# Layer 3, near tiles: VectorE masks all of the first pair of heads while ScalarE copies from the second, then both change banks

## The chip, the core and the metric

The kernel runs on one core of a Trainium2 chip. The metric is the time of one execution on the device in microseconds, the median of several. The core has five engines with queues of their own, each of which works strictly in the order in which its instructions were issued: TensorE (PE, with its weight loads shown apart as PEld), VectorE (DVE), ScalarE (ACT), GpSimd (POOL) and SyncE (SP), which issues the transfers. TensorE writes its results to PSUM, from where VectorE and ScalarE take them to SBUF.

## The reference

Four layers over x of shape (4, 256, 48, 48). Each adds to x a function of its group-normalised self; layers 0 to 2 are convolutions. The change is in layer 3, a linear attention over windows with 8 heads of 32 channels, for three window sizes:

```python
q = sigmoid(Wq x);  k = sigmoid(Wk x);  v = (Wv x) / |Wv x|      # per head
Ik, Ikv = integral(k), integral(k v^T)       # sums over rows and columns
for w in (1, 2, 4):                          # window of 48/w by 48/w pixels
    wk, wkv = box(Ik, 48 // w), box(Ikv, 48 // w)
    attn = einsum("bdhw,bdfhw->bfhw", q, wkv)
    norm = einsum("bdhw,bdhw->bhw", q, wk)
    outs.append(attn / (norm + 1e-6))
out = Wout concat(outs) + bout
```

The kernel doesn't form `k v^T` for each pixel. It computes the products q.k of a block of queries with a block of keys, sets to zero those in which the key lies outside of the query's window (the masks), and multiplies by v. One such product with three masks serves the three windows. The windows nest: with half sizes of 24, 12 and 6 pixels, everything in the smallest lies in the middle one, and everything in that lies in the widest.

## The kernel before

A tile is a block of 8 rows of keys (`a`) with one of three groups of 16 columns (`c`), 128 keys in all, against a block of 8 rows of queries (`rb`). There are 720 tiles in the kernel's order. Four heads are worked on in a tile, as two pairs. The scores of a pair fill a PSUM tile of two banks, one for each head; there are two such tiles, one for each pair, so that the scores of the next tile's first pair have to wait until the first pair of this one has been read.

```python
HALVES = [24, 12, 6]          # W // w // 2
LAG = 2

# ps_s: bufs=2, space=PSUM;   smp: bufs=2 * (LAG + 1)
def scores(self, pr, a, c):
    ...
    s = ps_s.tile([P, 2, 512], F32, tag="s", name="s")
    for j in range(2):
        head = slice((2 * pr + j) * D, (2 * pr + j + 1) * D)
        pe.matmul(s[:, j, 0 : (r1 - r0) * (c1 - c0)],
                  kvs[self.b, self.ct, a][0][head, c, :],
                  self.qs[head, r0:r1, c0:c1], start=True, stop=True)
    ...

def masked(self, a, c, ss):
    ...
    def of_banks(s, tiles, wi, rows, cols):      # VectorE: PSUM times mask -> SBUF
        src = s[:, :, rows[0] - r0 : rows[1] - r0, cols[0] - c0 : cols[1] - c0]
        times_mask(dve, wi, rows, cols, view(tiles, wi, rows, cols), src)

    f0, f1 = max(0, c * KC + KC - HALVES[0]), min(W, c * KC + HALVES[0] + 1)
    full = abs(a - rb) * RB + RB <= HALVES[0]    # no row of the widest window is cut
    many = seen(NW - 1, a, rb)                   # the smallest window reaches this tile

    def middle(s, tiles):                        # VectorE, the middle window
        if full and many:
            of_banks(s, tiles, 1, rows_seen(1, a, rb), cols_seen(1, c))

    def copy(s, tiles):                          # ScalarE, where the widest mask is all ones
        if full:
            act.copy(view(tiles, 0, (r0, r1), (f0, f1)), s[:, :, :, f0 - c0 : f1 - c0])

    def widest(s, tiles):                        # VectorE, the rim of the widest window
        if not full:
            of_banks(s, tiles, 0, *all0)
            return
        for p0, p1 in ((c0, f0), (f1, c1)):
            if p0 < p1:
                of_banks(s, tiles, 0, (r0, r1), (p0, p1))

    first, second = zip(ss, pairs)
    copy(*first)
    middle(*second)
    copy(*second)
    middle(*first)
    widest(*first)
    widest(*second)
    for tiles in pairs:                          # GpSimd, from what was copied to SBUF
        wi = NW - 1 if many else 1
        if wi in wis:
            rows, cols = rows_seen(wi, a, rb), cols_seen(wi, c)
            src = view(tiles, 0, rows, cols)
            times_mask(pool, wi, rows, cols, view(tiles, wi, rows, cols), src)
    ...

# the main loop: scores and masks of tile n, then the sums over keys of tile n - 2
for n in range(len(stream) + LAG):
    if n < len(stream):
        ...
        ss = [blocks[i].scores(pr, a, c) for pr in range(NPR)]
        ahead.append(blocks[i].masked(a, c, ss))
        ...
    if n >= LAG:
        ...
        for wi in (1, 0, 2):
            if wi in sms[0]:
                blocks[i].sums(wi, a, c, sms)    # TensorE: acc += v^T sm
        ...
    advance()       # a step of each side job: projections, sums of k, norms, outputs
```

A tile is near when `full and many` holds, that is when its block of rows is that of the queries or a neighbour (384 tiles). In a near tile VectorE makes the middle window and the rim of the widest (one piece for c = 0 and c = 2, two for c = 1), ScalarE copies what no mask cuts, and GpSimd makes the smallest window out of the copy. In 192 more tiles, two rows of blocks away, `full` holds and `many` does not; 144 are not `full`. Near tiles and others alternate as far as there are enough of the latter.

Two engines that read the same PSUM tile do so one after the other, in the order of the program: the framework that places the semaphores orders any two accesses to one bank.

Of the kernel before, what the change touches and what calls it, by code (L numbers as in the profile page):

```python
# [145 lines left out]
def conv_preact_kernel(  # L146
# [306 lines left out]
    with (  # L453
# [975 lines left out]
        with (  # L1429
# [11 lines left out]
            first = ExitStack()  # L1441
# [41 lines left out]
    with (  # L1483
# [187 lines left out]
        def rows_seen(wi, a, rb):  # L1671

            h = HALVES[wi]
            return (
                max(0, a * RB - h + 1 - rb * RB),
                min(RB, a * RB + RB + h - rb * RB),
            )

        def cols_seen(wi, c):
            h = HALVES[wi]  # L1680
            return max(0, c * KC - h + (wi > 0)), min(W, c * KC + KC + h)

        class Block:
# [28 lines left out]
            def masked(self, a, c, ss):  # L1712

                rb = self.rb
                all0 = rows_seen(0, a, rb), cols_seen(0, c)
                (r0, r1), (c0, c1) = all0
                wis = [wi for wi in range(NW) if seen(wi, a, rb)]
                pairs = [
                    {
                        wi: smp.tile(  # L1720
                            [P, 2, RB, min(W, KC + 2 * HALVES[wi])],
                            F32,
                            tag=f"sm{wi}",
                            name=f"sm{wi}",
                        )
                        for wi in wis
                    }
                    for _ in ss
                ]

                def view(tiles, wi, rows, cols):
                    (y0, _), (x0, _) = rows_seen(wi, a, rb), cols_seen(wi, c)
                    return tiles[wi][
                        :, :, rows[0] - y0 : rows[1] - y0, cols[0] - x0 : cols[1] - x0
                    ]

                def times_mask(engine, wi, rows, cols, dst, src):
                    mr = rb * RB + rows[0] - (a * RB - HALVES[wi] + 1)
                    mc = cols[0] - (c * KC - MCOL0[wi])
                    nr, ncol = rows[1] - rows[0], cols[1] - cols[0]  # L1740
                    m = mask[wi][:, mr : mr + nr, mc : mc + ncol]
                    engine.tensor_mul(
                        dst, src, m.unsqueeze(1).to_broadcast([P, 2, nr, ncol])
                    )

                def of_banks(s, tiles, wi, rows, cols):
# [6 lines that stand above are left out]
                full = abs(a - rb) * RB + RB <= HALVES[0]  # L1753

                many = seen(NW - 1, a, rb)

                def middle(s, tiles):
                    if full and many:
                        of_banks(s, tiles, 1, rows_seen(1, a, rb), cols_seen(1, c))

                def copy(s, tiles):
                    if full:
                        act.copy(
                            view(tiles, 0, (r0, r1), (f0, f1)), s[:, :, :, f0 - c0 : f1 - c0]
                        )

                def widest(s, tiles):
# [7 lines that stand above are left out]


                first, second = zip(ss, pairs)
                copy(*first)
                middle(*second)
                copy(*second)  # L1780
                middle(*first)
                widest(*first)
                widest(*second)
                for tiles in pairs:

# [5 lines that stand above are left out]
                return [  # L1791
                    {wi: view(t, wi, rows_seen(wi, a, rb), cols_seen(wi, c)) for wi in wis}
                    for t in pairs
                ]
# [28 lines left out]
        def seen(wi, a, rb):  # L1823
            r0, r1 = rows_seen(wi, a, rb)
            return r0 < r1
# [226 lines left out]
```

## Time and profile before

| | before |
|---|---|
| time, median of 3 runs | 3778.4 us (3774.7 to 3779.35) |
| span of the profiled execution | 3775.4 us |
| mean granted TensorE clock | 0.952 |
| busy: TensorE matmul, weight load | 3264.8 us (86%), 1879.4 us (50%) |
| busy: VectorE, ScalarE, GpSimd | 2487.2 us (66%), 1036.2 us (27%), 1518.1 us (40%) |
| VectorE masks of scores, `sm<-s,masks` | 2592, 1135.8 us busy |
| ScalarE copies of scores, `sm<-s` | 1152, 594.9 us busy |
| GpSimd masks, `sm<-sm,masks` | 1152, 853.3 us busy |

In the profile an instruction's operands carry the program's names: `s` is a PSUM tile of scores, `sm` one of the masked tiles in SBUF, `acc` the sums, `ks`, `qs` and `vs` are keys, queries and values. All instructions stand at one line of the program, L142, the helper that records them, so they are told apart by engine, operands and shape. `x <- y` in a list of waits reads "x sat idle until y was done"; after the colon stand the sum of these waits in us, their number and the longest. An fp32 matmul shows as two records.

### The profile page before, as it was taken

Reading aid. Unit: us, or ns where it says so; the run is one execution under the profiler, and the core shown is the slowest. Engines: PE = TensorE matmul, PEld = TensorE weight load, DVE = VectorE, ACT = ScalarE, POOL = GpSimd, SP = SyncE. Lnnn points to the kernel's source line nnn. Section 1 sums busy time; section 2 is a strip of 40 time slices with the busy share of each in tenths; the row PEclk is TensorE's granted clock in tenths of the full one; section 3 lists DMA queues with packets and bytes.
Section 4 is the critical chain, followed back from the end, with each engine's and each line's share of the span. In section 5 each row is a group of like instructions: output and inputs, shape, how many; then the busy total and the mean of one; then the engine's idle time right before and its main releaser. Section 6 shows DMA issues by size and latency. Waiting matters only on the chain. (4 is left out here: it accounts for less than half of the span.)

```text
span 3775.4 us, 68847 instructions
## 1 busy us (share of the span) xinstructions
PE 3264.8 (86%) x26498; PEld 1879.4 (50%) x26498; DVE 2487.2 (66%) x5119; ACT 1036.2 (27%) x2025; POOL 1518.1 (40%) x2184
## 2 busy tenths in 40 slices
PE   3688898998996788988889889899899899989998
PEld 2467686786784564433334334344443344444443
DVE  7876587587583366777666567756577766556665
ACT  0012111111113322433222333332344332233331
POOL 0000120020020034778765486755365766344332
PEclk9798999999997899999999899999999999999999
DMA  7745323324324313345434243533223444101122
GB/s 250 238 135 170 100 104 116 109 95 125 109 75 124 102 70 108 125 136 159 125 103 131 90 136 122 164 97 108 78 95 123 139 116 116 47 31 53 41 60 60
DMA packets 373019, 423.04 MB, mean 112 GB/s; under 512 B 129076, under 2 KB 328532, under 8 KB 371540
## 3 DMA queue, kind: packets, MB, share of 16 engines
q1 hardware_dynamic: 371491, 416.32, 35.6%
q8 instruction: 211, 3.46, 0.4%
q0 software_dynamic: 144, 1.52, 0.2%
q14 instruction: 117, 0.95, 0.1%
q10 hardware_dynamic: 1056, 0.79, 0.1%
HBM read 288.79 MB, written 131.25 MB: 111 GB/s over the span
## 5 line engine op out<-in xcount | busy, mean ns | idle before, releaser
L142 DVE TENSOR_TENSOR sm<-s,masks 128x112 f32<-128x112 f32 (+10 forms) x2592 | 1135.8, 493 | 765.5 <-PE s L142 321.1
L142 POOL TENSOR_TENSOR sm<-sm,masks 128x432 f32<-128x432 f32 (+14 forms) x1152 | 853.3, 755 | 936.5 <-ACT sm L142 672.0
L142 PE MATMUL s<-qs,ks 32*128 32x320 f32 (+3 forms) x5760 | 832.5, 500 | 200.1 <-DVE sm L142 151.2
L142 ACT COPY sm<-s 128x528 f32<-128x528 f32 (+2 forms) x1152 | 594.9, 535 | 1470.7 <-PE s L142 1169.9
L142 PE MATMUL acc<-sm,vs 128*32 128x384 f32 (+18 forms) x13440 | 880.5, 385 | 16.1 <-POOL sm L142 15.8
L142 PEld LDWEIGHTS s<-qs,ks 32*128 32x128 f32 x5760 | 374.1, 185 | 604.7 <-DVE sm L142 232.8
L142 PE MATMUL cv<-vx,wt 128*128 128x288 f32 x2080 | 559.3, 425 | 90.7 <-DVE vx L142 49.1
L142 PEld LDWEIGHTS acc<-sm,vs 128*32 128x32 f32 x13440 | 355.2, 110 | 551.3 <-issue 348.6
L142 PEld LDWEIGHTS cv<-vx,wt 128*128 128x128 f32 x2080 | 402.4, 198 | 212.4 <-issue 53.6
L142 POOL MEMSET v<- 128x16 f32 (+1 forms) x120 | 18.6, 215 | 725.7 <-DVE vx L142 635.7
L142 PE MATMUL cv<-v,wl 128*128 128x384 f32 x1152 | 224.5, 354 | 24.4 <-DVE x L142 9.2
L142 PEld LDWEIGHTS cv<-v,wl 128*128 128x128 f32 x1152 | 214.8, 195 | 34.6 <-issue 16.1
L142 POOL TENSOR_TENSOR pt<-pt 128x144 f32<-128x144 f32 x336 | 187.4, 558 | 22.8 <-DVE pt L142 0.5
L142 POOL TENSOR_TENSOR v<-l2v,v 128x384 fp32r<-128x384 f32 x96 | 109.2, 1168 | 130.2 <-ACT v L142 121.4
L142 POOL TENSOR_TENSOR nhi<-nhi,nq 128x384 f32<-128x384 f32 x144 | 148.3, 1058 | 0.0
L142 PE MATMUL cv<-pad,wl 128*128 128x384 bf16 x864 | 143.1, 327 | 0.0
L142 PE MATMUL out_ps<-o,wout_sb 128*128 128x384 f32 x288 | 122.8, 509 | 9.4 <-DVE o L142 5.4
L142 PE MATMUL out_ps<-stage,wout_sb 128*128 128x384 f32 x288 | 117.3, 489 | 0.4 <-DVE stage L142 0.4
L142 PE MATMUL proj_ps<-wv_sb,xn 128*128 128x256 f32 x288 | 89.5, 438 | 32.3 <-ACT vt L142 19.1
L142 DVE TENSOR_TENSOR vx<-v 128x868 f32<-128x868 f32 x112 | 115.4, 1056 | 0.5
L142 PE MATMUL ap<-seen,xT 120*128 120x120 f32 (+3 forms) x832 | 113.5, 293 | 0.0
L142 PEld LDWEIGHTS <-wl 128*128 128x128 bf16 x864 | 83.8, 97 | 59.1 <-issue 0.4
(162 smaller groups left out, 2859.0 us busy)
## 6 DMA issues: line engine op xcount, KB each, us to landing
wt<-wt SPq DMA_DIRECT2D x48, 768.0 KB
kb_d<-pt SPq DMA_DIRECT2D x48, 576.0 KB
rc<-r_d SPq DMA_DIRECT2D x192, 144.0 KB
nhi<-kb_d SPq DMA_DIRECT2D x120, 192.0 KB
nlo<-kb_d SPq DMA_DIRECT2D x88, 192.0 KB
o_d<-stage SPq DMA_DIRECT2D x24, 576.0 KB
o<-o_d SPq DMA_DIRECT2D x24, 576.0 KB
wl<-wl_d SPq DMA_DIRECT2D x16, 768.0 KB
```

What stands on the lines that cost most here:

```text
L142: return lambda *args, **kwargs: self.tc.keep_in_program_order(op(*args, **kwargs))
```

## The change

In near tiles the order of the six steps is changed. Before, ScalarE began with the first pair and VectorE with the second, and they changed pairs after one step. Now VectorE does its whole work on the first pair (middle and rim) while ScalarE copies from the second; then ScalarE copies from the first, and VectorE does its whole work on the second. The thought behind it is that VectorE can begin when the first pair's scores are there, without waiting for the second's, and that it comes to be done with the first pair's banks sooner. For the other tiles the order stays what it was: `middle` did nothing there.

```diff
                 first, second = zip(ss, pairs)
-                copy(*first)
-                middle(*second)
-                copy(*second)
-                middle(*first)
-                widest(*first)
+                if full and many:
+                    middle(*first)
+                    widest(*first)
+                    copy(*second)
+                    copy(*first)
+                    middle(*second)
+                else:
+                    copy(*first)
+                    copy(*second)
+                    widest(*first)
                 widest(*second)
                 for tiles in pairs:
```

## The prediction

> **What bounds the kernel now.** I read the page first, then the busy time by stretches, then the chain of waits of the stretch in which layer 3 runs, then one tile of it in order of time. The score matmuls, which the page calls `s<-qs,ks`, run from 1429.5 us to 3751 us, so layer 3's attention lies in the last 2327 us, and only there can the change act. The busy time of that stretch (us; then busy time and number of instructions of PE, PEld, DVE, ACT, POOL; clock, DMA share, GB/s):
>
> ```profile
> core 0: us, PE busy (x) PEld busy (x) DVE busy (x) ACT busy (x) POOL busy (x), PEclk, DMA share, GB/s
> 1429.00:3756.00 2327.00, 2071.52 (x20642) 938.44 (x20642) 1543.81 (x3288) 773.85 (x1537) 1364.18 (x1886) 0.97 0.34 103
> ```
>
> TensorE is busy 89% of it, VectorE 66%, GpSimd 59%, ScalarE 33%. TensorE is idle for 2327.0 - 2071.5 = 255.5 us, and the chain of waits of the same stretch says for whom (total us, times, longest):
>
> ```profile
> POOL sm L142 <- ACT sm L142: 672.0, 468, 18.0
> DVE sm L142 <- PE s L142: 321.1, 342, 9.2
> DVE sm L142 <- ACT sm L142: 266.9, 181, 5.5
> ACT sm L142 <- DVE sm L142: 235.9, 349, 3.8
> PE s L142 <- DVE sm L142: 151.2, 243, 3.9
> PEld acc L142 <- POOL sm L142: 57.7, 118, 3.8
> PE acc L142 <- POOL sm L142: 15.8, 17, 3.3
> PE s L142 <- ACT sm L142: 13.7, 20, 1.4
> ```
>
> The line to see is `PE s <- DVE sm`: 243 times TensorE cannot begin the scores of the next tile, because VectorE is still masking the banks they go into; 151.2 us, 59% of its idle time. GpSimd, which comes last in the masking, holds TensorE back for only 15.8 us. So the loop that sets the pace is scores, masking, release of the banks, next scores.
>
> One near tile in order of time (start, us, engine, operation, count, idle before it and what ended it):
>
> ```profile
> 2821.34 1.29 PE L142 MATMUL s<-qs,ks 32*128 32x384 f32 x8 [0.21 <-DVE sm L142]
> 2821.58 0.80 DVE L142 TENSOR_TENSOR pt<-cs 128x384 f32<-128x384 f32 x1
> 2822.36 0.61 ACT L142 COPY sm<-s 128x528 f32<-128x528 f32 x1 [0.87 <-PE s L142]
> ...
> 2822.75 2.28 DVE L142 TENSOR_TENSOR sm<-s,masks 128x624 f32<-128x624 f32 x6 [0.37 <-PE s L142]
> 2823.05 0.82 POOL L142 TENSOR_TENSOR sm<-sm,masks 128x324 f32<-128x324 f32 x1 [0.21 <-ACT sm L142]
> 2823.65 0.61 ACT L142 COPY sm<-s 128x528 f32<-128x528 f32 x1 [0.68 <-DVE sm L142]
> ...
> 2824.80 1.29 PE L142 MATMUL s<-qs,ks 32*128 32x384 f32 x8 [0.83 <-DVE sm L142]
> ```
>
> The first pair's scores can be read at 2822.36 (ScalarE starts on them), the second pair's at 2822.75 (VectorE starts on them, after 0.37 us of waiting for TensorE). VectorE runs m2, m1, w1, w1, w2, w2 back to back in 2.28 us (m is the middle window, w the rim of the widest, the digit the pair). ScalarE's second copy starts at 2823.65, 0.10 us after m2 is over (2822.75 + 0.80, the duration from the list below): the two engines are never in the same pair's banks together. The next scores start at 2824.80 after 0.83 us of idle TensorE, and the trace has the last w1 end 0.15 us before.
>
> VectorE's masks by shape (count, busy us, mean ns, idle before):
>
> ```profile
> L142 DVE TENSOR_TENSOR sm<-s,masks 128x624 f32<-128x624 f32 x256 | 194.9, 802 | 98.3 <-PE s L142 94.2 <-ACT sm L142 3.2 <-POOL sm L142 0.8
> L142 DVE TENSOR_TENSOR sm<-s,masks 128x448 f32<-128x448 f32 x256 | 147.9, 619 | 89.0 <-PE s L142 87.6 <-ACT sm L142 0.8
> L142 DVE TENSOR_TENSOR sm<-s,masks 128x432 f32<-128x432 f32 x256 | 143.7, 602 | 92.8 <-PE s L142 85.2 <-POOL pt L142 3.6 <-POOL sm L142 3.1
> ```
>
> These three are the middle masks of the three key columns c = 1, 0, 2, two to each near tile: 384 near tiles. Before them VectorE waits 94.2/128 = 0.74, 0.68 and 0.67 us a tile for TensorE. In all of these tiles it begins with the pair that is scored last.
>
> **What the Trainium skill says.** "PSUM — Partial Sum Buffer", section "PSUM bank collisions raise a hardware error", says that no two engines may be in one bank's quadrant at once, two readers included, and that software has to order them. The trace agrees: each `ACT sm <- DVE sm` (349 waits, 235.9 us) is a copy that waits for a mask of the same pair. So in the changed kernel the copy of the first pair has to follow w1, and m2 has to follow the copy of the second. "Perfetto Trace Analysis", section "Identifying the Most-Contended Engine", calls matmul busy time a bad measure of how near an engine is to its limit. Here too: the loads are busy 938 of 2327 us, 40%, while the matmul row shows 89%, and in 482 of the 719 steps from tile to tile the scores start within 0.3 us of VectorE's last mask on their banks. I therefore count waits and not busy shares.
>
> **The change part by part.** Nothing is added or removed: 2592 masks, 1152 copies and 1152 GpSimd products stay, each on its engine and with its shape. Only the order in the 384 near tiles changes. In the other tiles m was empty, so the order there is the same.
>
> For the tile above, with its own durations, the new order gives:
> - VectorE is free at 2821.58 + 0.80 = 2822.38, and the first pair is readable: it starts 0.37 us earlier. m1, w1, w1 are half of 2.28 us: over at 2823.52.
> - ScalarE copies the second pair from 2822.75 to 2823.36. That is before 2823.52, so m2 does not wait. The copy of the first pair starts 0.10 us after w1, at 2823.62, and ends at 2824.23.
> - The first pair's banks are then free, and 0.15 us later, at 2824.38, the next scores start, against 2824.80: 0.42 us earlier. TensorE has been free since 2823.97, so 0.41 of the 0.83 us stay.
> - m2, w2, w2 end at 2824.66 instead of 2825.03. With 0.15 us the second pair's banks are ready at 2824.81; the second scores follow the first by 0.40 us, at 2824.78. The second release takes nothing back.
>
> In general the first release moves from d + m2 + m1 + w1 to d' + m1 + w1 + c1. The gain is (d - d') + m - c - 0.10: the earlier start (about 0.4 us), one m (0.73, 0.56, 0.55 us when pipelined) less one copy (0.61, 0.51, 0.48 us) and one handover. That is 0.40 to 0.45 us with an idle VectorE. Where VectorE is busy with side work when the first pair is ready (a quarter of the tiles by its idle time ahead of m2), d - d' shrinks; c = 0 and 2 lose up to 0.3 us on m2 waiting for the copy. I take 0.35 us.
>
> It counts only where TensorE waits, and no more than the wait. I put the 243 + 20 waits of scores for VectorE and ScalarE beside the order of tiles: behind a near tile there are 86 (c = 1, 79.9 us), 57 (c = 2, 24.6 us) and 11 (c = 0, 9.0 us). The rest, over 100, stand behind other tiles, whose order stays. Taking the smaller of the wait and 0.35 us in each of the 154 gives 30.1 + 19.8 + 3.6 = 53.5 us. Behind the other 230 near tiles TensorE still had sums, projections or outputs to do, so the earlier release is not used.
>
> **What it costs.** GpSimd takes the pairs in the order first, second, and its input is the copy. The first copy now ends last: in the example at 2824.23 instead of 2822.97. GpSimd starts 1.2 us later, and ends near 2825.9 instead of 2825.15, and its own side work waits behind it. The sums that need these products come two tiles later: measured, they start 4 to 6 us (median) after the product is ready, but in 18 of 764 cases less than 1 us. Some 15 to 30 of these may now hold TensorE for 0.3 to 0.5 us: about 8 us. Net: 53.5 - 8 = 45 us, 1.2%: 3778.4 - 45 = 3733, rounded to 3732.
>
> **Rivals.** (a) GpSimd becomes the last wait. For it: its 672 us of waiting for ScalarE shows that it follows the copies closely, and it is 59% busy. Each near tile costs it about 1 us more of blocked time, 384 us in all, and 2327 - 1364 = 963 us are idle. Against it: the margins above. It would eat all of the gain: 3770 to 3800. (b) ScalarE blocks. It now waits for w1 with its first copy in hand, so sigmoid, stage and projection evacuations stand behind it; TensorE waits for these some 50 us today. Against it: the last copy ends at the same time as before (2824.23 against 2824.26). It would cost 10 to 20 us. (c) The whole wait goes: if the earlier VectorE also shortened the waits behind other tiles, up to 100 us might come, 3680. Against it: there the release follows the tile's own copies and masks, which do not move. (d) Nothing: TensorE's rate is the bound and the gain reappears as another wait, 3775. Against it: nearly all transitions start at a release.
>
> **Range and chances.** A gain of 0.25 us instead of 0.35 a wait, with the GpSimd loss doubled, leaves about 20 us; 0.45 us without loss gives 65. Unknown knock-on effects widen this to 3695 to 3775. Over 2% faster (below 3702.8) needs 0.5 us at each of the 154 waits, more than the arithmetic yields: 0.11. Over 2% slower needs GpSimd to take the lead outright: 0.06. Within: 0.83.
>
> **What would show it.** `PE s <- DVE sm` should fall from 151 us to 60 or less; part of it returns as `PE s <- ACT sm`, as a copy now frees the bank, and their sum (165 us) should come down by about 50. `DVE sm <- PE s` should fall from 321 us by about 0.4 us a near tile. `POOL sm <- ACT sm` should rise and `PE acc <- POOL sm` should stay below 30 us; if that reaches 60, rival (a) is right. Durations of masks and copies should not move. I am wrong if the first copy does not follow w1 at 0.1 us, or if the sum of scores' waits stays.

## The result, and the profile after

| | before | after |
|---|---|---|
| time, median of 4 runs each | 3776.55 us (3771.95 to 3779.35) | 3749.91 us (3744.02 to 3755.96) |
| ratio after to before, 95% interval | | 0.9931 (0.9911 to 0.9950) |
| span of the profiled execution, clock | 3775.4 us, 0.952 | 3748.1 us, 0.950 |

The change makes the kernel 26.6 us faster, 0.7%. In a second comparison, below, the ratio was 0.9920.

Layer 3 of the changed kernel by stretches; the first is batches 0 to 2, the second batch 3, cut where the trace has the first scores of a batch (us, busy us and number of instructions of PE, PEld, DVE, ACT, POOL, clock, DMA):

```profile
1422.05:3228.33 1806.29, 1624.76 (x15641) 723.96 (x15641) 1261.61 (x2591) 607.90 (x1210) 1166.03 (x1598) 0.96 0.39 118
3228.33:3722.00 493.67, 478.45 (x4962) 217.23 (x4962) 322.34 (x695) 160.70 (x324) 209.18 (x288) 0.99 0.17 49
```

The same two stretches of before:

```profile
1429.52:3233.67 1804.15, 1598.95 (x15640) 719.89 (x15641) 1228.40 (x2591) 609.88 (x1210) 1156.06 (x1598) 0.97 0.39 118
3233.67:3751.00 517.33, 469.32 (x4956) 217.01 (x4960) 313.19 (x695) 162.53 (x324) 208.13 (x288) 1.00 0.16 47
```

Batch 3 came down by 23.7 us. Batches 0 to 2, with three times as many tiles, came down by nothing (+2.1 us). Ahead of layer 3, where nothing was changed, this pair of traces differs by 7.5 us more, and behind these stretches by 1.7 us the other way: layer 3 began at 1429.5, 1422.0 and, in a third trace, at 1420.6 us, so that part is chance.

The clock plays a part too. The trace lists the phases in which TensorE's clock was halved; half of their length is called lost clock below. I read it as the most that such phases cost. In batches 0 to 2 it was 58.0 us before and 67.7 us after, in batch 3 1.7 and 3.4 us.

The chain of waits of layer 3 after:

```profile
POOL sm L142 <- ACT sm L142: 406.4, 200, 19.4
DVE sm L142 <- ACT sm L142: 296.3, 263, 7.3
DVE sm L142 <- PE s L142: 207.9, 200, 10.4
ACT sm L142 <- DVE sm L142: 98.0, 194, 3.2
PEld acc L142 <- POOL sm L142: 83.3, 142, 5.1
PE s L142 <- ACT sm L142: 66.7, 115, 3.4
PE s L142 <- DVE sm L142: 52.7, 98, 4.6
PE acc L142 <- POOL sm L142: 19.2, 21, 4.6
```

TensorE's waits ahead of scores for VectorE and ScalarE together fell from 151.2 + 13.7 = 164.9 us to 52.7 + 66.7 = 119.4 us. That is 45.5 us less: 30.8 us in batch 3 (from 44.0 to 13.2) and only 14.7 us in batches 0 to 2 (from 120.9 to 106.2). The kernel became less than 30 us faster. The page's own row for the scores tells where a part of the rest is. Before, then after (busy us, mean ns, idle before):

```profile
L142 PE MATMUL s<-qs,ks 32*128 32x320 f32 (+3 forms) x5760 | 832.5, 500 | 200.1 <-DVE sm L142 151.2
```

```profile
L142 PE MATMUL s<-qs,ks 32*128 32x320 f32 (+3 forms) x5760 | 861.2, 500 | 134.8 <-ACT sm L142 66.7
```

The same 5760 records of 500 ns each cover 28.7 us more time: they are stretched apart. One near tile (c = 1, the same in both traces) shows how. Before:

```profile
3329.37 1.29 PE L142 MATMUL s<-qs,ks 32*128 32x384 f32 x8
...
3330.78 2.28 DVE L142 TENSOR_TENSOR sm<-s,masks 128x624 f32<-128x624 f32 x6 [1.09 <-PE s L142]
...
3332.83 1.29 PE L142 MATMUL s<-qs,ks 32*128 32x384 f32 x8 [0.83 <-DVE sm L142]
```

After:

```profile
3318.02 1.20 PE L142 MATMUL s<-qs,ks 32*128 32x384 f32 x8
...
3319.06 2.28 DVE L142 TENSOR_TENSOR sm<-s,masks 128x624 f32<-128x624 f32 x6 [0.80 <-PE s L142]
...
3319.32 0.61 ACT L142 COPY sm<-s 128x528 f32<-128x528 f32 x1 [1.53 <-PE s L142]
3320.28 0.61 ACT L142 COPY sm<-s 128x528 f32<-128x528 f32 x1 [0.34 <-DVE sm L142]
3320.94 1.45 PE L142 MATMUL s<-qs,ks 32*128 32x384 f32 x8 [0.39 <-ACT sm L142]
```

Counted from the tile's own first scores, VectorE begins at 1.04 instead of 1.41 us, and the next scores begin at 2.92 instead of 3.46 us, 0.54 sooner, released by ScalarE's copy. But the group of eight now takes 1.45 instead of 1.29 us. It ends at 4.37 instead of 4.75: 0.38 us sooner, as much as VectorE's last mask. In the trace the second pair's scores start 0.15 us after that mask in both kernels: 0.38 us after the first pair's before, 0.54 us after.

VectorE's middle masks after (count, busy us, mean ns, idle before):

```profile
L142 DVE TENSOR_TENSOR sm<-s,masks 128x624 f32<-128x624 f32 x256 | 205.2, 802 | 71.0 <-PE s L142 59.0 <-ACT sm L142 5.7 <-POOL sm L142 2.8
L142 DVE TENSOR_TENSOR sm<-s,masks 128x448 f32<-128x448 f32 x256 | 158.3, 618 | 60.1 <-PE s L142 43.2 <-ACT sm L142 14.8
L142 DVE TENSOR_TENSOR sm<-s,masks 128x432 f32<-128x432 f32 x256 | 154.0, 602 | 60.6 <-PE s L142 45.8 <-ACT sm L142 9.6 <-POOL pt L142 3.5
```

The mask takes what it took. The wait for the first scores has shrunk from 94.2 to 59.0, 87.6 to 43.2 and 85.2 to 45.8 us, and for c = 0 and 2 (448 and 432 elements) there is now some waiting for ScalarE: m2 for the copy of the second pair.

### The profile page after: what moved, and what is told of

It reads as the page before. It is cut to its first block, busy times and chain, and to the rows that moved or that the text cites. A ratio compares the mean times of both kernels' runs of the same rounds, so it can differ in the third digit from the quotient of the medians.

```text
span 3748.1 us, 69137 instructions
## 1 busy us (share of the span) xinstructions
PE 3291.0 (88%) x26498; PEld 1878.5 (50%) x26498; DVE 2529.4 (67%) x5119; ACT 1032.1 (28%) x2025; POOL 1528.8 (41%) x2184
## 3 DMA queue, kind: packets, MB, share of 16 engines
q8 instruction: 212, 3.47, 0.4%
## 5 line engine op out<-in xcount | busy, mean ns | idle before, releaser
L142 DVE TENSOR_TENSOR sm<-s,masks 128x112 f32<-128x112 f32 (+10 forms) x2592 | 1148.2, 492 | 695.4 <-ACT sm L142 296.3
L142 POOL TENSOR_TENSOR sm<-sm,masks 128x432 f32<-128x432 f32 (+14 forms) x1152 | 881.2, 787 | 910.8 <-ACT sm L142 406.4
L142 PE MATMUL s<-qs,ks 32*128 32x320 f32 (+3 forms) x5760 | 861.2, 500 | 134.8 <-ACT sm L142 66.7
L142 PE MATMUL acc<-sm,vs 128*32 128x384 f32 (+18 forms) x13440 | 886.4, 386 | 19.5 <-POOL sm L142 19.2
L142 DVE TENSOR_TENSOR pt<-cs 128x384 f32<-128x384 f32 x144 | 120.3, 835 | 0.0
L142 DVE SCALAR_TENSOR_TENSOR x<-cv,alpha,x 128x384 f32<-128x384 f32 x144 | 83.9, 610 | 44.6 <-PE cv L142 44.3
```

The costliest lines, as they stand in the source:

```text
L142: return lambda *args, **kwargs: self.tc.keep_in_program_order(op(*args, **kwargs))
```

## The experiments

Each ratio is to the kernel before, run on the same chip. "VectorE's end" is, from the trace, the median over the 384 near tiles of the time from the tile's first scores to the end of VectorE's last mask of it.

| kernel | median us | ratio (95% interval) | VectorE's end, us |
|---|---|---|---|
| before | 3776.1 to 3781.7 | 1 | 3.30 |
| changed, again | 3744.9 | 0.9920 (0.9899 to 0.9942) | 3.10 |
| GpSimd second pair first | 3738.5 | 0.9897 (0.9876 to 0.9918) | 3.08 |
| begin with the first pair only | 3813.9 | 1.0096 (1.0066 to 1.0126) | 3.37 |
| changed order without w2 | 3712.2 | 0.9835 (0.9810 to 0.9860) | 2.86 |
| order of before without w2 | 3731.5 | 0.9874 (0.9846 to 0.9903) | 2.95 |
| mirror image | 3790.6 | 1.0028 (1.0016 to 1.0040) | 3.32 |
| first release later | 3783.1 | 0.9998 (0.9988 to 1.0009) | 3.16 |
| second release later | 3801.2 | 1.0053 (1.0037 to 1.0068) | 3.47 |
| crossing order two rows away | 3746.8 | 0.9913 (0.9896 to 0.9930) | 3.08 |
| the same and GpSimd second pair first | 3732.2 | 0.9876 (0.9856 to 0.9895) | 3.06 |
| that, and the second pair's rim by ScalarE and GpSimd | 3736.5 | 0.9890 (0.9872 to 0.9908) | 2.86 |
| the same in batch 3 alone | 3723.3 | 0.9855 (0.9832 to 0.9878) | 2.95 |

The last column was found after the runs. It orders most of the kernels as the times do. Two exceptions are the two slowest, which change places, and the run with GpSimd's rim in all batches, which is as early as the changed order without w2 (2.86 us) and 24 us slower. The run with the first release later is also slower than its 3.16 us would have it. So an early end of VectorE is not enough by itself.

**The changed kernel again.**

> The changed kernel once more, so that the others can be compared with it on one chip, and to see how far its trace repeats. All theories: 3742 to 3758 us, 26 us under the kernel before. If the gain sits where the first trace has it, batches 0 to 2 of layer 3 come out within 8 us of before and batch 3 some 24 us shorter.

From first scores to first scores batches 0 to 2 took 1803.6 us (before 1804.2), batch 3 with its last tile's scores 490.1 (before 517.0). So the empty gain in the first three batches is no accident of one trace. The lost clock there was 64.3 us.

**GpSimd takes the second pair first.**

```diff
-                for tiles in pairs:
+                for tiles in pairs[::-1] if full and many else pairs:
```

> The changed order, but in near tiles GpSimd multiplies the second pair first, whose copy ends first. GpSimd theory (the late first copy holds up GpSimd, its side work and the sums, and that ate the missing half of the gain): the waits of sums for GpSimd fall from 19 us to under 12, those of the norms from 12 to 10, and the kernel is 8 to 20 us faster than the changed one, 3730 to 3742. Second-bank theory (the second pair's banks come free too late to use the first release): within 4 us of the changed kernel.

6.4 us faster than the changed kernel by the medians, 0.0023 or 8.7 us by the ratios; the intervals overlap, but the same edit on top of the crossing order, below, gave 0.0037. The mean granted clock over the runs was no higher (0.9503 against 0.9513), so it does not explain the gain. In the traces the gain lies in batches 0 to 2 (1784.7 us against 1803.6), and not in batch 3 (489.5 against 490.1). That is where the GpSimd theory puts it, since there GpSimd has its side work; but of these 18.9 us up to 13.8 are less lost clock (50.5 against 64.3 us). The signature that I had named didn't come: the sums still wait 18.6 us for GpSimd. What did change is the length of GpSimd's own masks, 787 ns in the changed kernel, and here as before:

```profile
L142 POOL TENSOR_TENSOR sm<-sm,masks 128x432 f32<-128x432 f32 (+14 forms) x1152 | 851.7, 757 | 892.6 <-ACT sm L142 696.3
```

and the length of VectorE's side work, whose two inputs both lie in SBUF. Before, after, and this run:

```profile
L142 DVE TENSOR_TENSOR o<-o,rc 128x384 f32<-128x384 f32 x69 | 58.1, 841 | 0.0
L142 DVE TENSOR_TENSOR stage<-stage,rc 128x384 f32<-128x384 f32 x69 | 47.9, 694 | 0.1
```

```profile
L142 DVE TENSOR_TENSOR o<-o,rc 128x384 f32<-128x384 f32 x72 | 67.7, 943 | 5.1 <-DMA rc<-r_d 5.1
L142 DVE TENSOR_TENSOR stage<-stage,rc 128x384 f32<-128x384 f32 x72 | 58.4, 814 | 1.0 <-DMA rc<-r_d 1.0
```

```profile
L142 DVE TENSOR_TENSOR o<-o,rc 128x384 f32<-128x384 f32 x72 | 62.3, 868 | 4.8 <-DMA rc<-r_d 4.8
L142 DVE TENSOR_TENSOR stage<-stage,rc 128x384 f32<-128x384 f32 x72 | 54.0, 752 | 1.0 <-DMA rc<-r_d 1.0
```

The Trainium skill, "SBUF — State Buffer", section "SBUF: two separate sides", says that a VectorE instruction with two SBUF inputs and a GpSimd instruction that reads SBUF lock each other out of a shared pair of ports for a whole instruction. The trace agrees: in the changed kernel the 5 of the 72 `o<-o,rc` that overlap no GpSimd instruction took 529 ns in the mean, the 63 that overlap GpSimd for over half of their time 997 ns. The rows of before leave out the last three products of each kind; with them its means are 829 and 688 ns. So 114 and 126 ns were added by the changed order, and half to two thirds of it went again. The masks of scores, with one input in PSUM, did not change (493, 492, 491 ns). That the collisions are what the gain of GpSimd's order consists of is not shown, and the length of these products does not order the kernels: in the run with the first release later, below, they take 770 and 678 ns, less than before.

**Begin with the first pair, but change after one step.**

```diff
                 if full and many:
                     middle(*first)
-                    widest(*first)
                     copy(*second)
                     copy(*first)
                     middle(*second)
+                    widest(*first)
```

> Only half of the change: VectorE begins with the first pair, but changes pairs after one step (m1, then m2, w1, w2; ScalarE copies the second, then the first). By the arithmetic of the prediction m2 has to wait for the copy of the second pair (about 0.35 us of idle VectorE), so that w1 ends where it did before: within 10 us of before, 3766 to 3786. If an early start of VectorE alone were the gain, 3750 or less.

36 us slower than before, outside of what I expected; but starting early brings nothing by itself, as the argument had it. VectorE starts at 0.98 us and ends at 3.37, later than before, as it waits for the copy of the second pair in the middle of its work. The idle time in this piece of the trace is that wait (448 elements is c = 0):

```profile
3375.45 0.62 DVE L142 TENSOR_TENSOR sm<-s,masks 128x448 f32<-128x448 f32 x1 [0.56 <-PE s L142]
...
3376.55 1.25 DVE L142 TENSOR_TENSOR sm<-s,masks 128x448 f32<-128x448 f32 x3 [0.48 <-ACT sm L142]
```

Both releases come later than before, by 0.13 us each for c = 0 and 0.06 us for c = 2 (medians). Some of the 36 us is the clock (see the last section). Whether these two make up the whole was not tested.

**Without the second pair's rim, in both orders.** These leave out part of the masking: the rim is copied unmasked.

```diff
-                    copy(*second)
+                    act.copy(view(second[1], 0, *all0), second[0])
                     ...
-                widest(*second)        # in near tiles
```

> The changed order without the second pair's rim mask in near tiles: ScalarE copies that rim unmasked (its copy gets longer), VectorE does m1, w1, m2. This leaves out part of the masking. Second-bank theory: the second release comes about 0.4 us sooner, the time from the first to the second scores behind a near tile goes back from 0.40 to 0.60 us to 0.37 to 0.40, and the kernel gains 20 to 30 us on the changed one (3720 to 3730). GpSimd theory: within 6 us of the changed kernel, as GpSimd's input comes no sooner.

> The control: the order of before with the same cut (the second pair's rim copied unmasked by ScalarE, w2 left out in near tiles). Second-bank theory: in the old order the second scores were not held back, so little comes of it: 0 to 8 us faster than before, 3768 to 3778. If less work for VectorE is what counts and not the release, it gains as much here as on the changed order, 20 us or more.

On the changed order: 33 us by the medians, as the second-bank theory said. But the control gained 47 to 50 us on the order of before, where that theory gave it 0 to 8 and the other reading, less work for VectorE, 20 or more. These two runs can't part the readings, since without w2 VectorE has less work and both releases come sooner in the control. What its trace does show is that the assumption behind the control was wrong, and it was the prediction's assumption too: in the old order the second scores *were* held back. In the tile shown above (c = 1) the control's next scores have this row:

```profile
3313.79 1.12 PE L142 MATMUL s<-qs,ks 32*128 32x384 f32 x8 [0.54 <-ACT sm L142]
```

They begin 3.16 us after the tile's first (3310.63), and take 1.12 us, against 3.46 and 1.29 in the kernel before. In the trace the second pair starts 0.21 us after the first, 0.06 us after VectorE's last mask; before, 0.38 us after the first, 0.15 us after that mask. So the second scores wait in the control too, only less. How they run when they do not wait can be read from the kernel before: in 224 of its groups both releases came at least 0.1 us ahead of the first scores, and there the two pairs start 0.01 us apart (median). One of these:

```profile
3313.95 0.93 PE L142 MATMUL s<-qs,ks 32*128 32x384 f32 x8
```

The same eight records take 0.93 us. The 0.40 us of the prediction were a wait and no rhythm.

**The mirror image.**

```diff
                 if full and many:
-                    middle(*first); widest(*first); copy(*second)
-                    copy(*first);   middle(*second)
+                    middle(*second); widest(*second); copy(*first)
+                    copy(*second);   middle(*first); widest(*first)
```

> The mirror image of the change: VectorE does all of the second pair while ScalarE copies the first, then both change. VectorE starts as late as before, and the first pair, which is needed first, comes free last: about 0.4 us later than before behind some 200 near tiles whose successor starts at the release. 60 to 80 us slower than before, 3836 to 3858. If only the number of changes of banks mattered, it would be as fast as the changed kernel, 3750.

9.5 us slower than before, where 60 to 80 were expected. The same tile:

```profile
3352.03 2.28 DVE L142 TENSOR_TENSOR sm<-s,masks 128x624 f32<-128x624 f32 x6 [1.09 <-PE s L142]
3352.33 0.82 POOL L142 TENSOR_TENSOR sm<-sm,masks 128x324 f32<-128x324 f32 x1 [0.53 <-ACT sm L142]
3353.30 0.61 ACT L142 COPY sm<-s 128x528 f32<-128x528 f32 x1 [1.05 <-DVE sm L142]
3353.97 0.69 PEld L142 LDWEIGHTS s<-qs,ks 32*128 32x128 f32 x8 [1.06 <-ACT sm L142]
3353.97 1.31 PE L142 MATMUL s<-qs,ks 32*128 32x384 f32 x8 [0.72 <-ACT sm L142]
```

The next scores start at 3353.97, when the *second* pair's copy is over (3353.91), while VectorE works on the first pair's banks until 3354.31. It is so in 197 of the 199 groups of scores that wait behind near tiles. So the next first pair doesn't have to use the banks of this first pair, against what was said ahead of the prediction. By what rule it is given its banks is not shown. Which pair is released first is of little account then; what is left is when the first and the last release come. Both come about as before here (3.30 and 3.69 us for c = 1, 3.32 and 3.70 before), and so does the time.

**Each release later by itself.**

```diff
                     copy(*first)
+                    act.copy(...)   # first: 8 columns of the first pair once more
                     middle(*second)
+                    of_banks(...)   # second: 8 columns of the second pair's rim once more
```

> The changed order, and in near tiles ScalarE copies 8 columns of the first pair a second time, with the same values: the first release comes some 0.25 us later (2.87 to about 3.12 us after the tile's first scores for c = 1), still before the second release (3.31), which stays. Last-release theory (the score group cannot end before the bank that comes free last, so that one sets the time): within 8 us of the changed kernel, 3740 to 3756. First-release theory, that of the prediction (the time follows the wait before the first scores): 0.25 us behind some 150 near tiles, 35 us or more slower, 3780 or above.

> The changed order, and in near tiles VectorE masks 8 columns of the second pair's rim a second time: the second release comes some 0.18 us later, the first release and everything on the first pair stay. Last-release theory: 0.18 us behind the 200 to 230 near tiles whose successor starts at a release, 30 to 40 us slower than the changed kernel, 3775 to 3790. First-release theory: within 8 us of the changed kernel, 3740 to 3756.

For c = 1 the delays were 0.30 us (the first release from 2.86 to 3.16) and 0.33 us (the second from 3.31 to 3.64). In the tile shown above the two theories part cleanly. First release later (tile at 3352.66):

```profile
3355.88 1.16 PE L142 MATMUL s<-qs,ks 32*128 32x384 f32 x8 [0.59 <-ACT sm L142]
```

Second release later (tile at 3357.08):

```profile
3359.99 1.78 PE L142 MATMUL s<-qs,ks 32*128 32x384 f32 x8 [0.39 <-ACT sm L142]
```

The group ends at 4.38 in the first (changed kernel 4.37), at 4.69 us in the second. Over all of layer 3 it is not so clean: by the ratios the delay of the first cost 0.0078, 29 us, that of the second 0.0133, 50 us. In batch 3, which is free of side work, they cost 8.1 us (498.2 against 490.1) and 20.1 us (510.2). So the last release weighs more, but the first is not free: neither theory holds alone. The clock is part of both costs. In batch 3 the lost clock was 0 with the first release later and 6.8 us of the 20.1 with the second later; in batches 0 to 2 the first release cost 34.0 us (1837.6 against 1803.6), of which up to 25.5 are lost clock (89.8 against 64.3). The two delays also load different engines, ScalarE and VectorE, and this was not separated.

**The crossing order in the other full tiles.**

```diff
+                elif full:
+                    copy(*first)
+                    widest(*second)
+                    copy(*second)
+                    widest(*first)
```

> The changed kernel, and in the 192 tiles two rows of blocks away VectorE takes the rim of the second pair while ScalarE copies the first, then they change; before, VectorE waited there for the first copy (begins 1.45 us after the tile's first scores instead of about 0.92). The last mask should end near 1.9 us instead of 2.26, the first release some 0.1 us later. Last-release theory: 0.15 to 0.3 us in some 150 of these tiles, 15 to 40 us faster than the changed kernel, 3705 to 3732. First-release theory: 5 to 15 us slower than the changed kernel, as the first bank comes free later.

> The changed order in near tiles with GpSimd taking the second pair first, and the crossing order in the tiles two rows away. If both gains are real they add up: 3700 to 3725. If the 8 us of the GpSimd order were drift of the clock, as fast as the crossing order alone.

No gain from the crossing: 0.9913 against 0.9920 for the changed kernel, though VectorE's last mask in these 192 tiles ends at 2.09 instead of 2.26 us (medians, from the traces). But the last release did not come sooner, since now ScalarE's second copy waits for VectorE and ends last. A tile with c = 2, first scores at 3274.59:

```profile
3275.92 0.76 DVE L142 TENSOR_TENSOR sm<-s,masks 128x256 f32<-128x256 f32 x2 [1.05 <-POOL sm L142]
3276.38 0.48 ACT L142 COPY sm<-s 128x384 f32<-128x384 f32 x1 [0.40 <-DVE sm L142]
3276.73 1.09 PE L142 MATMUL s<-qs,ks 32*128 32x384 f32 x8
```

VectorE is done at 3276.68, the copy at 3276.86. Over the 192 tiles the last of all the readers ends at 2.27 instead of 2.26 us, and the first release comes at 2.09 instead of 1.86 (medians; for c = 0 alone the last release came sooner, at 1.92). So both theories allow this result, and the run does not part them. The next scores take the first pair's banks here, although the second's last reader comes first in the program. GpSimd's order on top of it gave 0.9876, which confirms that edit a second time; some 4 of these 14 us are the clock (0.9508 against 0.9495 over the runs).

**The rim by ScalarE and GpSimd.** Complete masking again: ScalarE copies the second pair's rim, GpSimd masks it in SBUF.

```diff
-                    copy(*second)
+                    copy_all(*second)
                     ...
-                widest(*second)
+                times_mask(pool, 0, rim of second, in place)
```

> The fastest order so far (near tiles as changed, GpSimd second pair first, crossing order two rows away), and in near tiles the second pair's rim goes from VectorE to ScalarE and GpSimd: ScalarE copies it, GpSimd masks it in SBUF. VectorE's last mask ends some 0.3 us sooner, worth up to 30 us by the run without that rim; GpSimd gets 512 more products of 0.5 to 0.7 us, about 300 us more. If GpSimd has the room (it is busy 60% of layer 3): 3700 to 3720. If its lateness already costs time, as the 8 us from its order suggest: 3735 or more.

> The same in the last of the four batches alone, where GpSimd has next to no side work. 5 us or so faster than without, 3725 to 3735, under both readings; faster than the version with the rim moved in all batches if GpSimd is short of time in the first three.

In all batches: 3736.5 us, 0.9890 (0.9872 to 0.9908), no better than without. In the last batch alone: 3723.3 us, 0.9855 (0.9832 to 0.9878), the lowest ratio of a complete version in this study, although its interval overlaps those of others. By the traces batch 3 takes 480.3 and 480.2 us in the two (491.5 without), batches 0 to 2 take 1806.5 with the rim on GpSimd there, 1788.2 without. In batch 3 no lost clock is in the difference; in batches 0 to 2 up to 13.9 of the 18.3 us are (76.3 against 62.4 us). So the rim on GpSimd pays where GpSimd has no side work, and brings nothing in the other batches; that GpSimd lacks the time there is not shown.

## Why the prediction was right or wrong

The time, 3749.9 us, lies in the range, 18 us over the value given; "within 2%" was right. The mechanism was right as far as the first release goes, and left out the last. By its steps:

- *VectorE starts earlier, nothing waits for m2, the copy of the first pair follows w1.* Right for c = 1: the start came 0.37 us sooner, and of the 0.83 us that TensorE waited 0.39 stayed (predicted 0.41). ScalarE followed w1 after 0.03 us instead of 0.10, TensorE the copy after 0.05 instead of 0.15, so that the first release came 0.54 instead of 0.42 us sooner.
- *The sum of the scores' waits comes down by about 50 us,* from VectorE to 60 or less, part of it returning under ScalarE. Right: 45.5 us, 52.7 and 66.7. Behind near tiles the waits fell from 113.5 to 64.3 us, 49.2 where the prediction had 53.5.
- *"The second release takes nothing back."* This step failed. I had read the 0.40 us between the first and the second scores as the natural distance; it was itself a wait for VectorE's last mask, and groups of the same trace that wait for no release show 0.01. The next group cannot end before the last release, and that came sooner by no more than VectorE's whole work did. For c = 1 that is 0.38 us. For c = 0 and 2 m2 waits for the copy, which I had counted as a loss "up to 0.3 us" and then smoothed over with 0.35 us for all (its own sum gives 0.42, 0.35 and 0.37 us for c = 1, 0 and 2, not the "0.40 to 0.45" written there). Over all near tiles VectorE starts 0.44 us sooner and ends 0.20 sooner (medians). From first scores to first scores, the steps that begin in a near tile took 1529.8 us before, and 1483.0 and 1476.8 us in the two traces of the changed kernel: 47 and 53 us less, as predicted. But the steps that begin in other tiles took 25 and 26 us more (791.3 before, 816.2 and 816.9), for they begin with the groups whose first scores now come sooner while their second pair still waits. From the end of one group to the end of the next, the near steps came down from 1431.4 to 1407.7 and 1403.6 us: 24 to 28 us where the prediction had 53.5. This is the term that was mis-sized.
- *GpSimd costs 8 us.* The order of its pairs is worth 6 to 14 us in two comparisons, but not in the way predicted, so that the sizes agree is chance. The sums' wait for GpSimd rose from 15.8 to 19.2 us, not by 8. That of their weight loads rose from 57.7 to 83.3 us, but GpSimd's order left it at 79.9, so it is not what that order won. GpSimd's wait for ScalarE fell from 672 to 406 us instead of rising (its idle time ahead of masks stayed, 936 and 911 us, now put down to other releasers).
- *`DVE sm <- PE s` falls by 0.4 us a near tile,* 154 us: it fell by 113.
- *The rivals.* (a), GpSimd in the way, came true in part: the order of its pairs won 6 to 14 us. (b) and (c) were not seen. (d) came true in part: some of the shortened wait returned, not as another wait but inside of the score groups.

Why batches 0 to 2 gained nothing is only partly settled. The waits ahead of scores fell by only 14.7 us there, of which the late second pairs took a part back, and the lost clock was 6 to 10 us higher in the two traces of the changed kernel than before. GpSimd's place in the order is worth up to 19 us there in one pair of traces, most of which can be the clock; whether the rest comes by the ports or by its late side work was not told apart.

## What to carry to other kernels

When a producer fills two buffers in turn, look for the release that comes last: a wait that ends sooner ahead of the first may come back inside of the group, as rows that cover more time with the same mean, and not as idle time. A distance that looks like an engine's rhythm should be checked against groups that wait for no release; here the profile of before had 224 of them. When an edit brings one engine's last read forward, look whether another engine's read now ends last. And where an engine off the path reads what now comes last, change its order too; here one line added 0.2 to 0.4% to the 0.7 to 0.8% of the change.

## What was not expected of the hardware

- The granted TensorE clock differs between kernels that do the same work in another order. The run that begins with the first pair only had a mean of 0.9462 over its 4 runs, the kernel before 0.9505 on the same chip (11 runs). The changed kernel with one small instruction more in each near tile had 0.9458 (second release later, 4 runs) and 0.9478 (first release later, 20 runs), against 0.9502 for the kernel before (25 runs). A straight line through the runs of the kernel before gives 2.8 to 3.4 us for each thousandth, by the chip, so this is worth some 7 to 15 us between kernels. In the traces the clock is halved for multiples of 3.4 us; what sets off such a phase was not looked into.
- The score matmuls of the two pairs, on different rows of the array, start 0.01 us apart when both pairs' banks are free, and all eight records of 384 columns take 0.93 us; they take 1.12 to 1.78 us in the tiles shown in which the second pair's banks come late. The mean of one record does not show this: it is 500 ns before and after.
- VectorE's products with two SBUF inputs took 529 ns beside an idle GpSimd and 997 ns where GpSimd worked for over half of their time (`o<-o,rc`, changed kernel). By another order of GpSimd's masks alone their means changed by 62 to 75 ns.
